# Attention values brought back to queries by plain transposes, with ScalarE and VectorE adding the two halves of the keys, in the last two elements of a four-element transformer block

## The chip, the cores and the metric

One core of a Trainium2 chip runs the whole program. The metric is device time in microseconds (us) of one execution. The engines are named as the profile names them: PE is TensorE's matmul, PEld its weight load, DVE is VectorE, ACT is ScalarE, POOL is GpSimd, SP is SyncE, which issues the DMAs. Each has its own queue and works it off in order.

## The reference

Four batch elements of 512 tokens and 512 channels pass through two gated layers. The part that matters here is the second cross-attention, with 16 heads of 32 channels:

```python
q = _qdq(x) @ _qdq(wq).T + bq
kv = cond @ wkv.T + bkv
k, v = jnp.split(kv, 2, axis=-1)
...
attn = jax.nn.softmax(jnp.einsum('bnhd,bmhd->bhnm', q, k) * scale, axis=-1)
o = jnp.einsum('bhnm,bmhd->bnhd', attn, v).reshape(B, N, C)
out = _qdq(o) @ _qdq(wp).T + bp
...
x = x + jnp.tanh(g_xattn[0]) * _L0_xattn_ref(...)   # a recurrence over tokens
x = x + jnp.tanh(g_ffn[0]) * _L0_ffn_ref(...)       # 512 to 2048 to 512, one-bit weights
x = x + jnp.tanh(g_xattn[1]) * _L1_xattn_ref(...)   # the attention above
x = x + jnp.tanh(g_ffn[1]) * _L1_ffn_ref(...)       # one 512x512 layer, ternary weights
```

All is in float32; `_qdq` rounds each row to 8-bit steps, and 512 tokens attend to 512 keys.

## The kernel before

The four elements run through four layers each as generators, which the function `run` at the end of the kernel interleaves by place numbers: while element b is in attention, element b+1 is in its feed-forward. For the last element nothing is left to run beside its attention; the flag `alone` (line 838) says so. The instructions' order within an engine's queue is set when the program is built, by priority and modelled readiness, so it can differ from the order in which they are written.

The attention of an element (`attention_layer`, line 831) has 16 units: eight pairs of heads, and for each pair two halves of the queries (256 tokens). Its loop at line 1057 is a pipeline of three stages. In step k, unit k gets its scores, unit k-1 is turned, and unit k-2 has its values formed and collected:

- `scores` (927): per head i and query tile t, one matmul of 128 queries by 512 keys into `s_ps` (PE), the row maximum `at_nm` (DVE, line 938), the exponentials `at_P` with their sum (ACT, line 940).
- `turned` (948): four 128x128 transposes into `pt_ps` (PE), copied to SBUF as `at_PT`, by ACT (line 960), or, when `alone` and for the second head, by DVE (line 958). The PSUM ring for `pt_ps` is "acc" with two banks when alone, else "m" with three.
- `values` (962): 8 matmuls, which the profile shows as 16 instructions, into `o_ps`. Its 128 partitions are (i, a, d): head i of the pair, half a of the keys, channel d. The two halves of the keys stay apart here, and their columns are 256 queries. ACT copies it to `at_os` (line 980), a tile with one buffer.
- `collect` (982): brings this back to queries on the partitions. Two matmuls, one per query tile, take `at_os` as the weights and `comb` as the moving operand. `comb` (line 95) is 128x64, with ones at (i, a, d) against (i, d), so that one matmul turns and adds the two halves of the keys. Each shows in the profile as two loads and two matmul instructions. The result `ot_ps` (128 queries by 2x64) is multiplied by the reciprocal `at_rt` of the softmax sums into `at_o` (DVE, line 998).

`ot_ps`, `o_ps` and, outside of `alone`, `pt_ps` come from the ring "m" of three PSUM banks, as do `tp_ps`, `qr_ps`, `q_ps`, `p_ps` and `f_ps` of the other stages. `ff_hp` and `ff_acc` are the feed-forward's matmuls; `ff_z` and `qg_i` its gate and rounding. After the units, `project_out` (1015) rounds `at_o`, turns it (`qr_ps`) and projects it (`p_ps`), and `ternary` (1103) applies the last layer (`f_ps`). The helpers `matmul` and `transpose` record all matmuls under line 168 and all transposes under line 171.

Of the kernel before, what the change touches and what calls it, by code (L numbers as in the profile page):

```python
# [10 lines left out]
F32 = mybir.dt.float32  # L11
# [5 lines left out]
ALU = mybir.AluOpType  # L17
# [4 lines left out]
P = 128  # L22
# [8 lines left out]
def kernel(  # L31
# [36 lines left out]
    nc = tc.nc  # L68
    NB, T, D = x.shape
    FF = w1.shape[0]  # L70
    NT, NC, NF = T // P, D // P, FF // D
    NH, DH = 16, 32
# [8 lines left out]
    sm = ctx.enter_context(tc.tile_pool(name="small", bufs=4))  # L81
# [6 lines left out]
    ident = cp.tile([P, P], F32, name="ident")  # L88
# [6 lines left out]
    comb = cp.tile([P, 2, DH], F32, name="comb")  # L95
# [37 lines left out]
    def psum_tile(name, tag, dtype=F32):  # L133
        pool, bufs = psum["now"]
        return pool.tile([P, D], dtype, name=name, tag=tag, bufs=bufs[tag])

    def bank(name, dtype=F32):

        return psum_tile(name, "m", dtype)
# [13 lines left out]
    def in_turn(ins):  # L153


        if "on" in turn:
            if "ahead" in turn:
                behind(ins, turn["ahead"])
            turn["last"] = ins
        return ins  # L160
# [6 lines left out]
    def matmul(*args, **kwargs):  # L167
        return in_turn(nc.tensor.matmul(*args, **kwargs))  # L168

    def transpose(*args):  # L170
        return in_turn(nc.tensor.transpose(*args))  # L171
# [659 lines left out]
    def attention_layer(b, xb, pool, tiles=range(NT)):  # L831
# [150 lines left out]
        def collect(k):  # L982

            p, h = units[k]
            os = out_s.pop(k)
            pt = bank("ot_ps")[:, 0:P]
            for t in range(2):
                matmul(
                    pt[:, t * 64 : (t + 1) * 64],
                    lhsT=os[:, t * P : (t + 1) * P],  # L990
                    rhs=comb.rearrange("p i d -> p (i d)"),
                    start=True,
                    stop=True,
                )
            rt = sm.tile([P, 2, 2], F32, name="at_rt", tag="at_rt")
            nc.vector.reciprocal(rt, sums.pop(k))
            at = tiles[0] + 2 * h
            nc.vector.tensor_tensor(
                o_all[:, at : at + 2, p * 64 : p * 64 + 64].rearrange(
                    "p t (i d) -> p t i d", d=DH  # L1000
                ),
                pt.rearrange("p (t i d) -> p t i d", i=2, d=DH),
                rt.unsqueeze(3).to_broadcast([P, 2, 2, DH]),
                ALU.mult,
            )
# [51 lines left out]
        for k in range(len(units) + 2):  # L1057
# [23 lines left out]
            if k > 1:  # L1081
                collect(k - 2)
            if now:
                p, h = units[k]
# [212 lines left out]
    for b in range(NB):  # L1297
# [8 lines left out]
        start = b + 1 + 4.95 / SLOTS  # L1306
# [62 lines left out]
```

## Time and profile before

| | |
|---|---|
| three timed runs | 1128.49, 1131.49, 1133.18 us (median 1131.49) |
| profiled execution | 1129.12 us, of which the span of instructions 1127.3 us |
| mean granted TensorE clock | 0.954 |
| busy, share of the span | PE 85%, PEld 60%, DVE 78%, ACT 64%, POOL 27% |
| collects of element 0 / 1 / 2 / 3 | 422 to 600 / 640 to 819 / 845 to 986 / 1004 to 1091 us |
| one unit to the next, collects of element 2 beside the feed-forward | 10 to 14 us |
| one unit to the next, most collects of element 3 | 5 to 6.5 us |
| ot_ps (64 collects) | 256 matmul instructions, median 275 ns each from start to modelled end |

A busy share is taken over the whole span, over stages with different limits. Matmul durations overlap, since they are pipelined; what a group of them costs is read from the chain of waits, which gives each piece only its own stretch of time. In that chain, "issue" is time in which the engine waited for nothing that the profile shows.

### The profile page before, as it was taken

The numbers are of one execution on the slowest core, as the hardware profiler recorded it, in microseconds if no ns is written. First come the engines' busy times: TensorE is split into PE (matmuls) and PEld (weight loads), VectorE is DVE, ScalarE is ACT, GpSimd is POOL, SyncE is SP. The second block draws the span as 40 slices with busy tenths as digits, with TensorE's granted clock in tenths as the row PEclk, the third lists the DMA queues.
The fourth block names the chain that finished last, engine by engine and source line by source line (L and its number), as shares of the span: only waits on it lengthen the run. The fifth ranks groups of instructions, "written<-read, shape, count | busy, mean of one in ns | idle before, by whom it ended". The sixth has DMA issues, their size and how long they took to land.

```text
span 1127.3 us, 16575 instructions
## 1 busy us (share of the span) xinstructions
PE 962.9 (85%) x5548; PEld 678.1 (60%) x5548; DVE 877.7 (78%) x1885; ACT 721.4 (64%) x1482; POOL 308.8 (27%) x301
## 2 busy tenths in 40 slices
PE   3878898988878978899998797999999899888983
PEld 2344565555546656676776475777777677555651
DVE  5857547769877799998769899978689766688776
ACT  5677655453224677667767676777676677877763
POOL 3821004333104143531215536212122400112000
PEclk9888999998888999999999999999999999998996
DMA  8188854443434654645555554464674572333401
GB/s 279 38 291 302 295 193 150 177 177 149 149 120 151 225 189 155 217 159 175 191 187 182 164 182 169 152 208 150 218 214 146 187 233 60 113 104 104 130 2 38
DMA packets 85668, 189.58 MB, mean 168 GB/s; under 512 B 12240, under 2 KB 36816, under 8 KB 74576
## 3 DMA queue, kind: packets, MB, share of 16 engines
q1 hardware_dynamic: 85584, 188.53, 49.7%
q8 instruction: 44, 0.72, 0.3%
q14 instruction: 40, 0.33, 0.1%
HBM read 148.65 MB, written 39.85 MB: 167 GB/s over the span
## 4 chain that ended last, share of the span: by engine, by line
PE 43%; DVE 29%; ACT 13%; issue 5%; POOL 4%; DMA 4%; SPq 1%; ACTq 0%; POOLq 0%; DVEq 0%
PE ff_hp L168 13%; PE ff_acc L168 6%; PE pt_ps L171 5%; PE o_ps L168 4%; DVE at_nm L938 3%; PE v_ps L168 3%; DVE wk_q L631 3%; PE s_ps L168 3%; ACT at_P L940 3%; DVE qg_i L671 2%; PE tp_ps L171 2%; ACT at_PT L960 2%; PE qr_ps L171 2%; ACT wk_e L603 1%; DMA wn<-in_L_ffn_w_dram 1%
## 5 line engine op out<-in xcount | busy, mean ns | idle before, releaser
L168 PE MATMUL ff_hp<-wT,xp 128*128 128x512 f32 x1024 | 272.3, 410 | 3.1 <-ACT at_P L940 2.1
L168 PEld LDWEIGHTS ff_hp<-wT,xp 128*128 128x128 f32 x1024 | 195.4, 195 | 51.9 <-ACT at_P L940 4.4
L940 ACT ACTIVATE at_P<-s_ps,at_nm 128x512 f32<-128x512 f32 x256 | 174.8, 690 | 64.8 <-DVE at_nm L938 63.4
L938 DVE TENSOR_REDUCE at_nm<-s_ps 128x1 f32<-128x512 f32 x256 | 165.8, 677 | 27.1 <-PE s_ps L168 26.7
L676 POOL TENSOR_TENSOR ff_z<-qg_b,qg_s 128x512 f32<-128x512 bf16 x64 | 71.2, 1112 | 378.9 <-ACT qg_b L675 326.3
L171 PE MATMUL pt_ps<-ident,at_P 128*128 128x128 f32 x1024 | 142.0, 279 | 12.5 <-ACT at_os L980 5.1
L960 ACT COPY at_PT<-pt_ps 128x512 f32<-128x512 f32 x224 | 125.0, 596 | 39.1 <-PE pt_ps L171 38.4
L171 PEld LDWEIGHTS pt_ps<-ident,at_P 128*128 128x128 f32 x1024 | 113.9, 141 | 54.7 <-issue 13.9
L168 PE MATMUL ff_acc<-wT,hr 128*128 128x512 f32 x512 | 136.7, 408 | 6.3 <-DVE hr L688 3.3
L168 PE MATMUL s_ps<-at_kR,at_qR 128*128 128x512 f32 x256 | 97.2, 448 | 19.9 <-ACT at_P L940 12.7
L168 PEld LDWEIGHTS ff_acc<-wT,hr 128*128 128x128 f32 x512 | 92.4, 190 | 27.4 <-DVE hr L688 4.6
L736 ACT ACTIVATE ff_z<-ff_hp,coef 128x512 f32<-128x512 f32 x64 | 43.9, 686 | 68.7 <-PE ff_hp L168 65.6
L168 PE MATMUL o_ps<-at_PT,at_V 128*32 128x256 f32 x1024 | 72.6, 397 | 1.6 <-ACT at_PT L960 0.9
L675 ACT CAST qg_b<-qg_i 128x512 bf16<-128x512 int8 x80 | 49.4, 617 | 34.2 <-DVE qg_i L671 24.7
L741 DVE SCALAR_TENSOR_TENSOR ff_z<-ff_hp,coef,ff_z 128x512 f32<-128x512 f32 x64 | 47.6, 744 | 28.3 <-PE ff_hp L168 28.1
L168 PE MATMUL v_ps<-wkvT,cT 128*128 128x512 f32 x128 | 63.4, 643 | 5.0 <-DVE wT L318 1.8
L168 PEld LDWEIGHTS s_ps<-at_kR,at_qR 128*128 128x128 f32 x256 | 45.6, 194 | 35.9 <-ACT at_P L940 20.7
L168 PE MATMUL k_ps<-cT,wkvT 128*128 128x512 f32 x128 | 62.3, 637 | 3.1 <-ACT cT L455 1.4
L737 DVE SCALAR_TENSOR_TENSOR ff_z<-ff_z,ff_hp 128x512 f32<-128x512 f32 x64 | 43.5, 679 | 25.7 <-ACT ff_z L736 25.7
L687 ACT CAST hr<-tp_ps 128x512 fp32r<-128x512 f32 x64 | 37.6, 588 | 33.9 <-PE tp_ps L171 33.9
L631 DVE RECIPROCAL wk_q<-wk_q 128x256 f32<-128x256 f32 x32 | 54.3, 1718 | 1.4 <-POOL wk_p L619 1.4
L171 PE MATMUL tp_ps<-ident,ff_z 128*128 128x128 f32 x256 | 40.3, 281 | 14.9 <-ACT at_PT L960 5.8
(177 smaller groups left out, 1749.7 us busy)
## 6 DMA issues: line engine op xcount, KB each, us to landing
wT<-wD SPq DMA_DIRECT2D x72, 1024.0 KB, 5.3
wn<-in_L_ffn_w_dram SPq DMA_DIRECT2D x18, 1024.0 KB, 7.3
at_kR<-kD SPq DMA_DIRECT2D x128, 128.0 KB, 3.5
at_qR<-qD SPq DMA_DIRECT2D x256, 64.0 KB, 2.2
wD<-wT SPq DMA_DIRECT2D x12, 1024.0 KB, 4.5
kD<-k_half SPq DMA_DIRECT2D x16, 512.0 KB, 3.3
qD<-at_half SPq DMA_DIRECT2D x32, 256.0 KB, 2.1
cn<-in_ctx_dram SPq DMA_DIRECT2D x8, 512.0 KB, 5.9
```

The lines of the kernel that those rows point to most:

```text
L168: return in_turn(nc.tensor.matmul(*args, **kwargs))
L171: return in_turn(nc.tensor.transpose(*args))
L631: nc.vector.reciprocal(half, half)
L675: nc.scalar.copy(qb, qi)
L676: nc.gpsimd.tensor_tensor(grouped(src), grouped(qb), s.unsqueeze(2).to_broadcast([P, NG, GS]), ALU.mult)
L687: nc.scalar.copy(part[:, 0, :], pt)
L736: nc.scalar.activation(z, hp, AF.Tanh, scale=coef[:, 0:1])
L737: nc.vector.scalar_tensor_tensor(z, z, 1.0, hp, ALU.add, ALU.mult)
L741: nc.vector.scalar_tensor_tensor(z, hp, coef[:, 1:2], z, ALU.mult, ALU.mult)
L938: nc.vector.tensor_reduce(nm, sp, AX.X, ALU.max, negate=True)
L940: nc.scalar.activation(lanes[k, i, t], sp, AF.Exp, bias=nm, accum_out=sums[k][:, t, i : i + 1],)
L960: made[k] = nc.scalar.copy(dst, blocks(pt))
```

## The change

In the attention of elements 2 and 3 (b > NB - 3, with NB = 4), `collect` no longer multiplies by `comb`. Two 128x128 transposes bring `at_os` to queries by (i, a, d), in 256 columns of the same PSUM bank. ACT copies the columns with a = 1 (128 of them, in runs of 32) to a tile in SBUF, `at_oa`, and DVE adds to them the columns with a = 0 from PSUM, in place. The multiply by the reciprocals then reads this SBUF tile instead of PSUM. `at_oa` has one buffer, under the tag of a small tile `w_part` that is used once when the weights are prepared. Elements 0 and 1 keep the matmuls with `comb`.

```diff
             os = out_s.pop(k)
-            pt = bank("ot_ps")[:, 0:P]
-            for t in range(2):
-                matmul(
-                    pt[:, t * 64 : (t + 1) * 64],
-                    lhsT=os[:, t * P : (t + 1) * P],
-                    rhs=comb.rearrange("p i d -> p (i d)"),
-                    start=True,
-                    stop=True,
-                )
+            if b > NB - 3:
+
+                pt = bank("ot_ps")[:, 0 : 2 * P]
+                for t in range(2):
+                    transpose(pt[:, t * P : (t + 1) * P], os[:, t * P : (t + 1) * P], ident)
+                pt = pt.rearrange("p (t i a d) -> p t i a d", i=2, a=2, d=DH)
+                added = sm.tile([P, 2, 2, DH], F32, name="at_oa", tag="w_part", bufs=1)
+                nc.scalar.copy(added, pt[:, :, :, 1, :])
+                nc.vector.tensor_tensor(added, pt[:, :, :, 0, :], added, ALU.add)
+                pt = added.rearrange("p t i d -> p (t i d)")
+            else:
+                pt = bank("ot_ps")[:, 0:P]
+                for t in range(2):
+                    matmul(
+                        pt[:, t * 64 : (t + 1) * 64],
+                        lhsT=os[:, t * P : (t + 1) * P],
+                        rhs=comb.rearrange("p i d -> p (i d)"),
+                        start=True,
+                        stop=True,
+                    )
             rt = sm.tile([P, 2, 2], F32, name="at_rt", tag="at_rt")
             nc.vector.reciprocal(rt, sums.pop(k))
```

## The prediction

> **What bounds the kernel now.** I read the page first (busy shares), then the busy table by stretches of time, then the chain of waits over the stretches in which elements 2 and 3 are attended to, and last the rows of the instructions that the change adds or takes out.
>
> ```profile
> PE 962.9 (85%) x5548; PEld 678.1 (60%) x5548; DVE 877.7 (78%) x1885; ACT 721.4 (64%) x1482; POOL 308.8 (27%) x301
> ```
>
> TensorE (PE) is the busiest, but 85% is an average. By stretches (columns: us, then busy time and count on PE, PE's weight loads, DVE, ACT, POOL, then the granted clock):
>
> ```profile
> 900.00:945.00 45.00, 44.07 (x291) 34.11 (x290) 27.24 (x54) 32.81 (x76) 4.18 (x4) 1.00 0.52 170
> 945.00:990.00 45.00, 37.73 (x288) 26.25 (x287) 30.41 (x76) 36.79 (x89) 3.98 (x4) 0.96 0.32 98
> 1050.00:1070.00 20.00, 18.08 (x154) 11.72 (x154) 15.83 (x30) 14.49 (x38) 0.00 (x0) 1.00 0.48 150
> 1070.00:1091.00 21.00, 18.57 (x158) 12.31 (x156) 14.07 (x28) 13.32 (x35) 0.00 (x0) 1.00 0.03 9
> ```
>
> The change touches 32 collects, those of element 2 (845 to 986 us) and of element 3 (1004 to 1091 us). Until 945 the feed-forward of element 3 fills PE to 98% (44.07 of 45). From 945 on no engine is full: PE has 84 to 90%, ACT 63 to 82%, DVE 67 to 79%, so a loop of latencies sets the pace. The chain of waits shows what is last at each collect (columns: start, us on the chain, who):
>
> ```profile
> 938.80 0.87 PE pt_ps L171 x8
> 939.67 0.39 PE ot_ps L168 x4
> 940.06 0.56 PE tp_ps L171 x4
> ...
> 953.55 1.07 ACT at_PT L960 x2
> 954.63 0.69 ACT at_P L940 x2
> ...
> 1010.17 0.20 DVE at_o L998
> 1010.36 0.61 DVE at_nm L938
> ...
> 1055.03 0.39 PE ot_ps L168 x4
> 1055.43 0.45 PE qr_ps L171 x4
> ...
> 1066.98 0.59 ACT at_PT L960
> 1067.56 0.69 ACT at_P L940 x2
> ```
>
> Three sorts of collect are seen: PE's own work on the chain (ot_ps, 0.39 us), the multiply at_o on the chain (DVE), and neither, with the chain on ACT's copies at_PT and exponentials at_P. Going through the chain from 826 to 1091 us collect by collect I count ot_ps on it 15 times before the last collect (14 pieces of 0.39 and one of 0.75, at 985 us, where the clock was halved), at_o 4 times (845, 878, 1010, 1026 us), and neither 12 times; in 10 of the 12 the chain is on ACT, in one on a DMA and in one on POOL. The last collect, behind which nothing is left of the loop, is a case by itself:
>
> ```profile
> 1090.15 0.38 ACT at_os L980
> 1090.58 0.67 PE ot_ps L168 x4
> 1091.27 0.29 DVE at_o L998
> ```
>
> **The change part by part.** *Removed from PE:* four ot_ps matmul instructions with their loads, 0.39 us on the chain. *Added to PE:* two 128x128 f32 transposes. The row for these is qr_ps on the same chain, four in 0.45 us, so two take 0.22. Saved: 0.17 us a collect. The 14 collects give 14 x 0.17 = 2.4 us and the one at half clock 0.75 / 2 = 0.3 (two instead of four, about half): 2.7 us less. At the other collects PE is not last, and the saving is worth nothing.
>
> *Added to ACT:* one copy of 128x128 f32 out of PSUM, waiting for the transposes. *Added to DVE:* one add of 128x128, an operand of it in PSUM, waiting for that copy. Their rows:
>
> ```profile
> L862 ACT COPY at_sxb<-sx_ps x16: 257/260/343, 352.7 to 971.9; 128x128 f32<-128x128 f32 x16
> L998 DVE TENSOR_TENSOR at_o<-ot_ps,at_rt x64: 265/280/292, 422.6 to 1091.3; 128x128 f32<-128x128 f32 x64
> ```
>
> So 0.26 us on ACT and 0.28 on DVE. The multiply now reads SBUF in place of PSUM; that is between 0.18 (the 128x32 add from SBUF that makes comb) and 0.28 us; I keep 0.28, which is the same size of tile. A handoff between engines is about 0.04 us ("issue" pieces of the chain such as that between 1090.53 and 1090.58).
>
> Where the multiply stands on the chain, the add stands there too: 4 x 0.28 = 1.1 us more. At the 10 collects on ACT the copy comes out of the queue close to at_P: behind it wait the exponentials, the copies at_PT and at_os and, until 945, the gates of the feed-forward; for those wait the next transposes pt_ps and the value matmuls o_ps. It costs between nothing (the exponentials are ready first and go first) and 0.26 + 0.04 = 0.30 us. At 1066.98 the copy at_PT ends at 1067.56, and the transposes, put where ot_ps starts at 1067.21, would end at 1067.21 + 0.11 + 0.27 (a transpose's pace and its row's duration) = 1067.59, so the two are close rivals for the slot; I take the middle, 10 x 0.15 = 1.5 us, and keep 0 and 3.0 as ends.
>
> In element 2 both at_PT copies are ACT's, 1.07 us together, and the new copy comes after them: the add can start about 0.5 us later than the multiply could before (at 940.23 after matmuls that end at 940.07; now after copies that end at 940.34, 0.26 of copy and 0.04). DVE's queue behind it holds at_nm, for which at_P waits. DVE was busy 27 of 45 us there, and that idle time hides most of it; where DVE is on the chain in that element (2 collects) the 0.5 is open to view. I take 0.5 us in all, with ends 0 and 16 x 0.5 = 8.
>
> The PSUM bank of ot_ps is held by the copy and the handoffs longer, some 0.4 to 0.9 us, of three banks; the next but two on that ring is two or more of PE's groups later (at 940 us tp_ps takes the next, o_ps the one after at 941.03, pt_ps the third at 942.03 while ot_ps would be free by 940.9). I cost it at nothing; if that cover is gone it is 0.4 us a collect. The buffer for the sum is one, but the collects are at least 2.4 us apart. No DMA is added and SP's queue is untouched.
>
> *The last collect:* its matmuls (0.67 us) become two transposes (0.67 - 0.22 = 0.45, from the four qr_ps that wait for at_o at 1092.53 and take 0.67), then come handoff, copy, handoff and add: 0.04 + 0.26 + 0.04 + 0.28 = 0.62. Net 0.40 us more, for nothing lies beside it.
>
> Sum: -2.7 + 1.1 + 1.5 + 0.5 + 0.4 = +0.8 us. The profiled execution took 1129.12 us (span 1127.3 and 1.8 around it), so it becomes 1129.9. The three timed runs have their median 2.4 us above that, at 1131.49, and the same difference put on them gives 1132.3.
>
> Transposes in the place of matmuls could also touch the clock. The row: from 1050 to 1091 us, where pt_ps is much of PE's work, the granted clock is 1.00, and four transposes run in 0.45 us; the clock fell to 0.50 only after PE had idled (0.15 us busy between 1031 and 1034 us, then 0.50). The Trainium skill, "TensorE: Matmul & The Clock Gate", Part 4 (PE-mode transpose), says on the contrary that transposes do not count as PE work in the same way and do not bring on the full clock. By it the new collects would push the clock towards half, and with the 36.7 us that PE is busy between 1050 and 1091 the loss could reach tens of microseconds; the row speaks against that, and the sum above goes by the row.
>
> **The rivals.** *Slower: the two new handoffs join the loop of element 3.* That loop runs PE to ACT or DVE and back, with no engine full; copy, handoff and add between the transposes and the next at_nm and at_P would be paid at each collect, 0.30 + 0.28 = 0.58 us. For all 15 of element 3 before its last: 8.7, with 0.4 at the end and less the 1.35 that PE saves in element 2 (6 x 0.17 + 0.33): +7.8, or 1139.2 us. For it: ACT's queue is where the chain goes whenever PE waits (at_PT, at_P), and these are in-order queues. Against: DVE and ACT are idle there for a fifth to a third of the time. It passes +5.7 us from about 11 of the 15 collects on. With the seven collects between 945 and 990 as well it would be +12, 1144.
>
> *Faster: PE is the one thread everywhere.* ot_ps is on the chain at 15 of 31 collects; if PE's order is what holds the others too, all 31 gain 0.17: -5.3, with the end +0.4, -4.9. A half-clock stage of 3.4 us does 1.7 us of work less; losing one of the two that lie between 980 and 1000 us makes it -6.6, or 1124.9. For it: PE at 98% until 945 us. Against: the waits of at_PT for pt_ps and the ACT pieces above.
>
> *The order changes.* The reciprocal at_rt is written ahead of the multiply but has run at 1004.20, after the at_o at 1004.00 and a collect early, so the queues' order is not the written one, and four instructions fewer and others more can shift it from 845 us on. That is why my range takes in lumps such as the wait of the queries' DMA on the chain (5.74 us at 836.68), which can grow or shrink.
>
> **How the numbers follow.** 0.5% is 5.7 us, about what a measurement of this kernel can tell from no change: below 1125.8 is faster, above 1137.1 slower. The forecast's own ends are -1.2 (both open costs at nothing) and +5.0 (3.0 for the copy, 0.2 us at each of 16 collects for the later add); it gets 0.46 and falls within; the slower rival 0.34; the faster one with its half-clock stage 0.20. The range from 1124.5 to 1142 leaves out about one in ten on each side: the case of all 22 late collects above (the open cost of the later add at its full 8 us, +8.3, is inside), and a lump that leaves on top of the faster rival below.
>
> **What would show it.** Right: PE's piece at collects on the chain falls from 0.39 to 0.22; a 0.26 us copy at_oa on ACT and an add of 0.28 on DVE 32 times each; the stretch from 900 to 945 gets 0.5 to 1 us shorter; the collects after 945 keep their periods of 5 to 6 us within 0.2; the last at_o comes 0.4 us later after its at_os. Wrong: at_oa or its add on the chain at most collects of element 3 (slower rival), periods there 0.17 shorter throughout (faster rival), ACT idle before at_oa by more than 0.2 us in the mean, pt_ps or o_ps waiting for the add (bank held), the clock at half where it was 1.00, or a time outside of 1124.5 to 1142 with the queues' orders changed.

## The result, and the profile after

The changed kernel takes 1140.7 us (median of six runs, 1136.0 to 1144.1) against 1131.5 before: a ratio of 1.0085, 95% interval 1.0055 to 1.0114, so 9.2 us slower. Its profiled execution took 1135.95 us with a span of 1134.2, 6.9 more than the span before.

The stretches of time (columns as in the prediction's table), first of the kernel before at the beginning of element 3, which the prediction left aside:

```profile
1010.00:1030.00 20.00, 18.78 (x156) 12.01 (x154) 18.25 (x52) 15.93 (x43) 1.62 (x3) 1.00 0.48 141
1030.00:1050.00 20.00, 16.02 (x111) 10.97 (x109) 14.68 (x42) 14.50 (x35) 6.44 (x6) 0.83 0.22 66
```

The same stretches of the changed kernel, and those that answer to the prediction's table:

```profile
900.00:945.00 45.00, 44.33 (x301) 33.80 (x296) 27.77 (x61) 31.58 (x76) 3.93 (x4) 1.00 0.54 173
945.00:990.00 45.00, 35.58 (x260) 23.35 (x261) 29.24 (x78) 36.92 (x93) 4.23 (x5) 0.95 0.32 96
...
1010.00:1030.00 20.00, 17.44 (x139) 11.39 (x142) 19.09 (x45) 17.57 (x47) 1.26 (x1) 1.00 0.44 126
1030.00:1050.00 20.00, 10.73 (x79) 7.27 (x78) 14.77 (x49) 11.01 (x27) 8.05 (x8) 0.74 0.21 60
1050.00:1070.00 20.00, 19.59 (x152) 12.46 (x155) 16.60 (x33) 16.22 (x45) 0.00 (x0) 1.00 0.40 119
1070.00:1091.00 21.00, 17.97 (x152) 11.49 (x142) 16.99 (x37) 15.76 (x44) 0.00 (x0) 1.00 0.21 64
```

VectorE was at 91% from 1010 to 1030 us before the change and is at 95% after. The stretch behind it, 1030 to 1050, is the one with a hole: PE falls from 16.0 to 10.7 us. The rows of PE's waits between 1005 and 1060 us name it (us in total, times, longest), first before, then after:

```profile
PE qr_ps L171 <- ACT tf_xn L246: 3.6, 1, 3.6
PE s_ps L168 <- ACT at_P L940: 1.0, 2, 0.7
```

```profile
PE qr_ps L171 <- ACT tf_xn L246: 8.1, 1, 8.1
PE s_ps L168 <- ACT at_P L940: 3.2, 5, 1.4
```

The largest is one single wait for tf_xn; PE's waits for the exponentials at_P grew too, by 2.2 us. The wait for tf_xn is PE standing, in order, at the transposes of element 2's last layer (`ternary`), whose input comes from VectorE's small layernorm instructions (the last is ln_r), POOL, VectorE and ACT. The timeline before:

```profile
1027.97 0.16 DVE L220 SCALAR_TENSOR_TENSOR ln_r<-mv,rs_y 128x4 f32<-128x4 f32 x1
1028.38 1.53 POOL L228 TENSOR_SCALAR tf_xn<-xb,ln_r 128x512 f32<-128x512 f32 x2 [20.89 <-PE pt_ps L171]
...
1030.60 0.56 PE L168 MATMUL ot_ps<-comb,at_os 128*128 128x64 f32 x4
...
1034.74 1.12 PE L171 MATMUL qr_ps<-ident,tf_xn 128*128 128x128 f32 x4 [3.59 <-ACT tf_xn L246]
```

And after:

```profile
1034.18 0.38 PE L171 MATMUL ot_ps<-ident,at_os 128*128 128x128 f32 x2
...
1035.06 0.15 DVE L220 SCALAR_TENSOR_TENSOR ln_r<-mv,rs_y 128x4 f32<-128x4 f32 x1
...
1035.47 1.52 POOL L228 TENSOR_SCALAR tf_xn<-xb,ln_r 128x512 f32<-128x512 f32 x2 [23.75 <-DVE at_rt L1007]
...
1042.65 1.11 PE L171 MATMUL qr_ps<-ident,tf_xn 128*128 128x128 f32 x4 [8.08 <-ACT tf_xn L246]
```

Before, ln_r ended 2.5 us ahead of the start of PE's last work (the ot_ps at 1030.60); after, it ends 1.0 us behind the start of the ot_ps at 1034.18. That is 3.5 us, and the way from POOL's start to PE's grew from 6.36 to 7.18 us. The two make 4.3 of the 4.5 us by which the wait grew; the rest is that the ot_ps itself is 0.18 us shorter.

The new instructions cost what their nearest rows said:

```profile
L993 ACT COPY at_oa<-ot_ps x32: 264/274/308, 843.8 to 1097.7; 128x128 f32<-128x128 f32 x32
L994 DVE TENSOR_TENSOR at_oa<-ot_ps,at_oa x32: 236/283/292, 845.1 to 1098.0; 128x128 f32<-128x128 f32 x32
L1009 DVE TENSOR_TENSOR at_o<-at_oa,at_rt x32: 242/283/725, 845.9 to 1098.4; 128x128 f32<-128x128 f32 x32
```

The last collect, from the chain of waits after:

```profile
1096.84 0.38 ACT at_os L980
1097.27 0.45 PE ot_ps L171 x2
1097.74 0.27 ACT at_oa L993
1098.04 0.29 DVE at_oa L994
```

### The profile page after: what moved, and what is told of

It is laid out like the page before. It is cut to its first block, busy times and chain, and to the rows that moved or that the text cites. A ratio compares the mean times of both kernels' runs of the same rounds, so it can differ in the third digit from the quotient of the medians.

```text
span 1134.2 us, 16475 instructions
## 1 busy us (share of the span) xinstructions
PE 957.9 (84%) x5457; PEld 671.6 (59%) x5484; DVE 885.8 (78%) x1917; ACT 727.1 (64%) x1514; POOL 308.3 (27%) x301
## 4 chain that ended last, share of the span: by engine, by line
PE 40%; DVE 28%; ACT 13%; issue 8%; DMA 5%; POOL 4%; SPq 1%; POOLq 0%; ACTq 0%; DVEq 0%
PE ff_hp L168 12%; PE ff_acc L168 6%; PE pt_ps L171 5%; ACT at_P L940 3%; PE v_ps L168 3%; DVE wk_q L631 3%; PE o_ps L168 3%; DVE at_nm L938 3%; PE s_ps L168 3%; ACT at_PT L960 2%; DVE qg_i L671 2%; PE qr_ps L171 2%; PE tp_ps L171 1%; DVE ff_z L741 1%; DMA wn<-in_L_ffn_w_dram 1%
## 5 line engine op out<-in xcount | busy, mean ns | idle before, releaser
L687 ACT CAST hr<-tp_ps 128x512 fp32r<-128x512 f32 x64 | 37.6, 588 | 31.9 <-PE tp_ps L171 31.5
```

The lines of the kernel that those rows point to most:

```text
L687: nc.scalar.copy(part[:, 0, :], pt)
```

## The experiments

Two theories stood at the start. *Loop theory* (the slower rival): copy, handoff and add are paid at each collect. *Background theory*: VectorE's queue is full at the start of element 3, the adds displace low-priority work, and PE pays in a lump where it waits for that work. All kernels below the first row were timed in five rounds. In the table, "stretch" is the last start minus the first start of the 32 copies at_os in elements 2 and 3, out of one profiled execution (253.6 us before, from 836.55 to 1090.15; 260.3 after, from 836.57 to 1096.84), and "wait" is PE's wait for tf_xn as above. "At equal clock" is an estimate that is explained below the table.

| kernel | ratio to before (95%) | stretch, us over before | wait, us | at equal clock, us over before |
|---|---|---|---|---|
| the change | 1.0085 (1.0055 to 1.0114) | +6.7 | 8.1 | +5.4 |
| in element 3 alone | 1.0039 (1.0021 to 1.0057) | +3.8 | 8.1 | +2.4 |
| in element 2 alone | 1.0040 (1.0017 to 1.0064) | +3.6 | 3.6 | +3.0 |
| transposes without copy and add | 0.9996 (0.9971 to 1.0020) | -1.2 | 3.8 | -0.8 |
| matmuls, with copy and add | 1.0115 (1.0084 to 1.0145) | +8.7 | 7.9 | +5.5 |
| the change, norm first | 1.0075 (1.0049 to 1.0102) | +3.0 | 0.7 | +5.2 |
| before, norm first | 1.0005 (0.9985 to 1.0024) | +2.0 | none | +1.8 |
| element 2, first nine collects | 1.0022 (1.0005 to 1.0039) | +1.4 | 3.6 | +1.4 |
| element 2, last seven | 1.0010 (0.9995 to 1.0025) | +1.3 | 3.6 | +1.8 |
| element 3, collects 6 to 14 | 1.0035 (1.0013 to 1.0057) | +0.6 | 3.6 | +1.4 |
| element 3, collects 0 to 5 | 1.0074 (1.0047 to 1.0101) | +6.0 | 8.1 | +4.8 |
| transposes and copy, no add | 0.9999 (0.9975 to 1.0023) | +0.3 | 1.4 | +0.1 |
| transposes and add, no copy | 1.0060 (1.0039 to 1.0080) | +5.1 | 8.1 | +4.0 |

A caution on single traces: in most of these kernels PE's clock is halved for 3.4 us or more near 894 us, in the profiled execution of the kernel before it is not. It happens in the kernel that changes nothing before 1004 us, too (element 3 alone: 3.4 us from 894.7), and costs about 1 us of the stretch. The kernel with the change in element 3's first six collects is 2.2 us behind at element 3's first at_os, ahead of anything that it changes, so some 2 us of a stretch can be chance.

The clock bears on the times as well. Among the 82 executions of the kernel before that were timed beside these kernels, the time follows the mean granted clock: 1127.5 us at 0.952 and 1139.5 at 0.942 are the ends, and a straight line through all gives 0.76 us for each 0.001. The six of the changed kernel had 0.9447 on the mean, the 82 had 0.9481, and the means of their times are 8.1 us apart; by that line 2.6 us go with the clock and 5.4 remain. The last column is this estimate for each kernel, good to about 1 us. It doesn't say that the 2.6 us are chance: at the wait for tf_xn the clock is halved for 10.2 us in the changed kernel's trace and for 6.8 in the one before, so part of the lower clock may come of the change itself. No run here parts the two.

**Element 3 alone.**

```diff
-            if b > NB - 3:
+            if b > NB - 2:
```

> The transposes with copy and add in element 3 alone (the condition is b > NB - 2); element 2 keeps the matmuls with comb. Background theory: in the first quarter of element 3 VectorE is full (19 of 20 us after the change), the adds push back the chain of small instructions that is element 2's last layernorm, and PE waits in order for its row, so most of the loss comes here: 3 to 6 us over before, with PE's wait at qr_ps<-tf_xn grown from 3.6 us to 6 or more. Loop theory (each collect of element 3 pays copy, handoff and add): +8 to +9 us, spread evenly, with units of element 3 some 0.5 us longer.

It costs 0.39%, 4.4 us, with the wait at its full growth (8.1 us). That is the lump of the background theory. The loop theory's even spread is not there: in this trace the start of o_ps lies 4.7 us later behind the wait than ahead of it, compared with before, and then comes back by 1.4 us over the last nine units.

**Element 2 alone.**

```diff
-            if b > NB - 3:
+            if b == NB - 2:
```

> The transposes with copy and add in element 2 alone (b == NB - 2); element 3 keeps the matmuls. Background theory: 0 to 4 us over before, from POOL's and VectorE's order in element 2 and a stage of half clock, and PE's wait at qr_ps<-tf_xn in element 3 stays within 1 us of the 3.6 us of before. Loop theory: 1 us less than before, since there the saving on PE is all that counts.

It costs 0.40%, 4.5 us, just above what the background theory allowed and against the 1 us less of the loop theory, and the wait stays as before (3.6 us). So half of the loss has nothing to do with that wait. The prediction's 1.35 us saved on PE in this element is not seen.

**Transposes without copy and add.**

```diff
-                added = sm.tile([P, 2, 2, DH], F32, name="at_oa", tag="w_part", bufs=1)
-                nc.scalar.copy(added, pt[:, :, :, 1, :])
-                nc.vector.tensor_tensor(added, pt[:, :, :, 0, :], added, ALU.add)
-                pt = added.rearrange("p t i d -> p (t i d)")
+                half_only = pt[:, :, :, 0, :]
```

> The transposes stay in elements 2 and 3, but copy and add are left out: the multiply reads the first half of the keys from PSUM and the second half is dropped. It shows what PE's saving is worth by itself. Both theories: faster than before, by 2 to 5 us (2.7 on the chain counted collect by collect, less about 0.2 at the end), with PE's wait at qr_ps<-tf_xn back at 3 to 4 us. If the transposes themselves cost more or bring the clock down, it is not faster.

Not faster by anything that can be measured (0.9996). The orders of ACT's, VectorE's and POOL's queues in this trace are the same as before, instruction by instruction, so it is the saving alone. Its chain of waits in element 2:

```profile
856.81 0.22 PE ot_ps L171 x2
857.03 0.11 issue
857.14 0.63 PE tp_ps L171 x4
...
867.19 0.22 PE ot_ps L171 x2
867.40 0.02 issue
867.42 1.02 PE q_ps L168 x4
```

The same two places before:

```profile
855.73 0.39 PE ot_ps L168 x4
856.12 0.57 PE tp_ps L171 x4
...
866.11 0.39 PE ot_ps L168 x4
866.50 0.87 PE q_ps L168 x4
```

0.22 + 0.11 + 0.63 = 0.96 against 0.39 + 0.57 = 0.96, and 1.26 against 1.26: PE starts the next group no sooner. In both kernels tp_ps starts 0.73 us after ACT began the copies at_PT (855.33 to 856.06 before, 856.41 to 857.14 here), and q_ps 0.63 us after. By the order of the ring the next group takes the PSUM bank that the first of these copies frees; the trace itself only calls the gap "issue", so the bank is the likely reason, not a shown one. What was on the chain as PE's work covered a gap. In element 3 most of the saving did come through in the trace: from its first at_os to its last 89.4 us instead of 90.4, 1.0 of the 1.4 counted (8 x 0.17).

**Matmuls with copy and add.**

```diff
-                    transpose(pt[:, t * P : (t + 1) * P], os[:, t * P : (t + 1) * P], ident)
+                    matmul(
+                        pt[:, t * 64 : (t + 1) * 64],
+                        lhsT=os[:, t * P : (t + 1) * P],
+                        rhs=comb.rearrange("p i d -> p (i d)"),
+                        ...
-                nc.scalar.copy(added, pt[:, :, :, 1, :])
-                nc.vector.tensor_tensor(added, pt[:, :, :, 0, :], added, ALU.add)
+                nc.scalar.copy(added, pt)
+                nc.vector.tensor_tensor(added, pt, added, ALU.add)
```

> The matmuls with comb stay in elements 2 and 3, and the copy on ScalarE and the add on VectorE are put behind them (the sum is added to its own copy, so the attention values are doubled). It shows what copy and add cost by themselves. Background theory: 8 to 13 us over before, in lumps, the largest at PE's wait for qr_ps<-tf_xn in element 3. Loop theory: 10 to 13 us, even over the collects after 945 us.

1.0115, 13 us: both theories' ranges hold it. With the lump again (wait 7.9 us), it fits the background theory, but it does not tell the two apart. It says that copy and add are enough for the whole loss, without the transposes.

**Norm first, in the changed kernel and in the one before.**

```diff
-        r = layernorm(xb, rms=True)
+        if b == NB - 2:
+            with tc.high_priority():
+                r = layernorm(xb, rms=True)
+        else:
+            r = layernorm(xb, rms=True)
```

> The changed kernel, with element 2's last layernorm (its statistics, the 13 small instructions of its root, its scales) put first in the queues as soon as its rows are there; nothing is left out. Background theory: PE's wait at qr_ps<-tf_xn in element 3 falls from 8.1 to 3 us or less, and with it the 4.7 us that the changed kernel lost at this place: 1.0085 of before becomes 1.003 to 1.005. Loop theory: copy and add are paid at each collect, whatever the order of the norm; the ratio stays at 1.007 to 1.0085.

> The kernel before with the same order of the norm, as the control of the last run: 1 to 4 us less than before, as far as PE's wait of 3.6 us at qr_ps<-tf_xn shrinks, since VectorE is full there in that kernel too (18.3 of 20 us). If the wait does not shrink, the norm's place is not what PE waits for.

The waits for tf_xn went, to 0.7 us in the changed kernel, to none in the other. Others came in their place; between 1005 and 1060 us, first the changed kernel with the norm first, then the control:

```profile
PE qr_ps L171 <- ACT tf_xn L246: 0.7, 1, 0.7
PE s_ps L168 <- ACT at_P L940: 5.4, 6, 1.6
```

```profile
PE s_ps L168 <- ACT at_P L940: 3.8, 5, 2.1
ACT at_P L940 <- DVE at_nm L938: 4.6, 4, 2.2
```

PE's wait for at_P was 1.0 us before the change and 3.2 after it, and ACT waited 1.6 and 1.7 us for VectorE's row maxima at_nm; now ACT waits 4.6 us for them in the control and 4.1 in the changed kernel. From the first to the last at_os of element 3 all waits of PE add up to 9.1 us before and to 9.0 in the control.

The time did not go down. The control ran at 1.0005, where 1 to 4 us less were forecast; the changed kernel at 1.0075, outside of what the background theory gave it and inside of what the loop theory gave it, with an interval that holds both 1.005 and the 1.0085 of the change. In the single trace its stretch is 3.7 us shorter than the change's, which the timed runs do not show. In the control's trace the starts of o_ps fall back by 4.9 us over the five units ahead of the old place of the wait, and by 4.7 us less right behind it. So the place of the norm decides where PE stands, not how long in all: the background theory, as an account by the order of the norm alone, fell here. What remains of it is that VectorE's queue has more to do than fits: with the norm first it is the row maxima that come late.

**Element 2 in two parts.**

```diff
-            if b > NB - 3:
+            if b == NB - 2 and k < 9:
...
+            if b == NB - 2 and k >= 9:
```

> The change in the first nine collects of element 2 alone, beside the feed-forward of element 3, where PE was 98% busy. The whole of element 2 cost 4.5 us. Order theory (VectorE's and POOL's queues are rearranged by the adds, PE's saving goes into a wait for at_PT's banks): 0 to 2 us over before, above all 0.9 us at the third collect. PE theory (PE sets the pace there): 1 to 1.5 us less than before.

> The change in the last seven collects of element 2 alone, when the feed-forward has ended and ScalarE makes both at_PT copies and the rounding of element 3's inputs. Order theory: 2 to 4 us over before, the rest of what element 2 cost, in PE's waits for ScalarE between 960 and 1000 us. PE theory: within 1 us of before.

2.5 us for the first nine, 1.1 for the last seven (which the interval does not part from nothing). The order theory had 0 to 2 and 2 to 4: both missed, though the intervals don't tell the two parts apart (1.4 and 1.8 at equal clock). The theory of PE setting the pace beside the feed-forward is out: nine collects with less work for PE, at 98% busy, made it slower. Together they give 3.6 of the 4.5 us.

**Element 3 in two parts.**

```diff
-            if b > NB - 3:
+            if alone and 6 <= k < len(units) - 1:
...
+            if alone and k < 6:
```

> The change in element 3 alone and only in its collects 6 to 14 (after the place where PE waits for element 2's last layer, and without the last collect); everything else as before. Theory of a full VectorE: VectorE has room here (67% busy), so PE's saving comes through: 1 to 1.5 us less than before, counted from collect to collect in the traces (0.9985 to 0.9990 in time, which is within what the runs can tell). Loop theory: 9 x 0.58 = 5 us more than before.

> The change in the first six collects of element 3 alone, in which VectorE is full. Theory of a full VectorE: nearly all of element 3's loss, 3 to 5 us over before, in one lump at PE's wait for qr_ps<-tf_xn (8 us in place of 3.6). Loop theory: 6 x 0.58 = 3.5 us, spread over the six units, the wait at qr_ps<-tf_xn as before.

The first six cost 0.74%, 8.4 us (5.3 to 11.4), with the lump (wait 8.1 us). The lump is what the theory of a full VectorE said, the size is not: it had 3 to 5 us, the loop theory 3.5. The late nine do not have the wait's growth, but they aren't free: 1.0035, about 4 us (1.5 to 6.5), where the theory of a full VectorE gave a gain of 1 to 1.5 and the loop theory 5 us more. In the trace their stretch is 0.6 us longer only, which speaks against the loop theory, and the saving that came back in the kernel with all of element 3 changed does not appear. At equal clock it's 1.4 us, so part of the 4 may be the clock. The parts don't add up to the whole either (8.4 and 4.0 against 4.4 for all of element 3; 4.8 and 1.4 against 2.4 at equal clock). This stays open. No version here beats the kernel before.

**Copy without add, add without copy.**

```diff
-                nc.vector.tensor_tensor(added, pt[:, :, :, 0, :], added, ALU.add)
...
-                nc.scalar.copy(added, pt[:, :, :, 1, :])
-                nc.vector.tensor_tensor(added, pt[:, :, :, 0, :], added, ALU.add)
+                nc.vector.tensor_tensor(
+                    added,
+                    pt[:, :, :, 0, :],
+                    ident.rearrange("p (t i d) -> p t i d", i=2, d=DH),
+                    ALU.add,
+                )
```

> The changed kernel without VectorE's add: ScalarE copies the second half, and the multiply reads this copy from SBUF; the first half of the keys is dropped. Theory of a full VectorE: PE's wait at qr_ps<-tf_xn falls back to 3 to 5 us and the loss to 0 to 3 us over before. If ScalarE's copy and its handoff are what costs, the loss stays at 6 to 9 us, and the wait at 8 us.

> The changed kernel without ScalarE's copy: VectorE adds a constant tile of the same size from SBUF to the first half in PSUM; the second half of the keys is dropped. Theory of a full VectorE: most of the loss stays, 4 to 8 us over before, and PE's wait at qr_ps<-tf_xn is 6 us or more. If the copy is what costs, the loss is 0 to 3 us and the wait 3 to 5 us.

This settles which of the two. With ScalarE's copy and its handoffs, but no add, nothing that can be measured is lost (0.9999, within 2.8 us either way) and the wait is shorter than before the change, and than the 3 to 5 us forecast:

```profile
PE qr_ps L171 <- ACT tf_xn L246: 1.4, 1, 1.4
```

With the add, but no copy, 0.60% is lost, 6.8 us (4.4 to 9.1), and the wait is full (8.1 us). At equal clock it is 0.1 against 4.0 us, the same answer. The loss comes with VectorE's add. The 2.4 us between this kernel and the change can't be told from nothing, since the two intervals overlap. How 0.28 us a collect becomes this much is shown in part only: the wait for tf_xn and the waits for at_P are seen to grow, but a kernel with an add also has its queues in another order, and no run adds work to VectorE without that.

## Why the prediction was right and wrong

The range (1124.5 to 1142) held the time; the likeliest case, no change that can be measured, was wrong, and the slower rival with its 0.34 came about, near its time (1139.2 against 1140.7). Its mechanism did not: it let each collect of element 3 pay 0.58 us for copy and add alike, and forecast less time in element 2, where half of the loss is. That its number is near is luck.

- *Instructions.* Transposes 0.22, copy 0.27 (0.26 forecast), add 0.283 (0.28), last collect: from the start of at_os to that of at_o 1.12 us before (1090.15 to 1091.27) and 1.56 after (1096.84 to 1098.40), 0.44 more (0.40 forecast). All right.
- *PE's saving, -2.7 us.* Mis-sized: 0.9996, some 0.5 us, and -1.2 in the trace. Of the 1.4 of element 3 1.0 came; the 1.35 of element 2 was booked because the chain ran over ot_ps, and it went into a gap ahead of the next group, most likely the wait for a PSUM bank that ACT's copies free.
- *The copy at 1.5 us.* By itself it costs nothing that can be measured (0.9999).
- *The add, 1.1 us on the chain and 0.5 behind the copies.* This is the step that failed. The prediction charged it at the four collects where at_o stood on the chain, and let VectorE's idle time hide the rest, "a fifth to a third", read from the stretches behind 1050 us and from 945 to 990. From 1010 to 1030 us, at the beginning of element 3, VectorE was at 91%. The add alone costs 6.8 us over the two elements, and with the copy 9.2.
- *The open cost of 16 x 0.5 = 8 us*, for the adds of element 2 that come late, was set at 0.5 us; element 2 costs 4.5 us.
- *The stretch from 900 to 945 shorter by 0.5 to 1 us, and the collects after 945 keeping their periods within 0.2:* neither came about. From 940.7 to 942.5 after, PE takes as long from pt_ps to s_ps (1.83 us) as before from 938.8 to 940.6 (1.82), and the period over the wait for tf_xn grew by 4.3 us (at_os to at_os, 11.2 to 15.5).
- *The clock.* From 1050 to 1091 us it is 1.00 with the transposes, as with the matmuls, and in the kernel with transposes alone from 1051 to 1091 also; the row that the prediction went by holds here, not what it drew from the Trainium skill, "TensorE: Matmul & The Clock Gate", Part 4 (PE-mode transpose), that the new collects would push the clock towards half. Transposes are 18.9 of the 37.6 us that PE is busy there, the rest is matmuls; a stage of transposes alone was not run.
- *"The order changes."* It did, from 844 us on, for ACT and VectorE, and from 859 us on for POOL, and the largest single hole, 4.5 us, is a background chain that fell behind. But the two kernels with the norm first show that the norm's place alone is not the price.

An observation with no proof of its own: if each add counted in full, at 0.283 us, the losses would be 9.1 us for all 32 (9.2 measured), 4.5 for each element (4.5 and 4.4), 2.5 for the first nine of element 2 (2.5), 2.0 for the last seven (1.1, within its interval) and 2.5 for the late nine of element 3 (4.0, within its interval). The first six of element 3 don't fit (1.7 against 8.4), nor do matmuls with copy and add (9.1 against 13, at the edge of the interval). At equal clock all 32 cost 5.4 us, so the agreement with 9.1 may well be luck.

## What to carry to other kernels

Look up the idle time that is to hide new work in the stretch where the work falls, not in a neighbour's or in a mean: an engine at 78% over the span was at 91% just there, and 0.28 us on it cost more than 0.17 us saved on the "busiest" one brought. A piece of the busiest engine on the chain of waits can cover a wait behind it; see what the next group needs (here most likely a PSUM bank that another engine frees) before its shortening is booked as gain. And where a queue is full, a background chain can give way in it (here a layernorm), so ask which in-order engine stands waiting for that; but putting that chain first won nothing here, since the row maxima then came late.

## What was not expected of the hardware

While POOL worked on tiles of 128x512, two instructions of VectorE with both inputs in SBUF were stretched: a 128x1 product (tf_s, 0.14 us elsewhere) took 1.22 us at 1040.36, beside POOL's instruction of 1.26 us from 1040.30, and one multiply at_o took 0.725 us instead of 0.283 at 1036.40, beside POOL's two instructions from 1035.47 to 1036.99. With an input in PSUM this was not seen: the add at_oa took 0.29 us at 1036.07 beside POOL, and in the kernel before, where the multiply reads PSUM, it took 0.28 us at 1032.44 beside POOL's instruction from 1032.34. So moving the multiply's input to SBUF had a price of its own, 0.44 us once in this trace.
